# Plain parts of a graph layer: the difference to the gathered rows as a PSUM product on TensorE instead of a subtraction on VectorE

## The chip, the core and the metric

One core of a Trainium2 chip. The metric is the device time of the whole program in microseconds: 2913.64, the median of three runs (2913.59 to 2916.97). The runs of the kernel before and of the changed kernel are compared on the same chip.

## The reference

One graph layer with 12,500 nodes of 128 features and 412,500 edges sorted by destination, followed by a residual and a layer norm:

```python
theta = x[dst] - x[src]
w = sigmoid(relu(theta @ W1 + b1) @ W2 + b2)
agg = segment_sum(w * theta, dst, n_nodes)
indeg = segment_sum(ones, dst, n_nodes)
x = layernorm(x + agg + indeg * (x @ W4 + b4))
```

For an edge the kernel needs relu(y[dst] + b1 - y[src]) with y = x @ W1, its product with W2, a sigmoid, and the weighted sums by destination.

## The kernel before, in words

**Table.** First the kernel computes a table z in DRAM with a row of 256 numbers a node: y = x @ W1 in the first 128, x in the last 128.

**Parts.** Edges are worked on in parts. Parts 0 to 17 are plain parts of 1024 edges each (`PLAIN` = 18, `early_part`); from part 18 on (`part`) 1532 edges make a part, of which up to 1024 are gathered and the rest are "hot" edges, whose source rows TensorE picks out of tables in SBUF (`tabs`, bf16 terms). For a part GpSimd issues eight gathers (`gather`, L404), one for each of eight tiles of 128 edges, into a buffer `zbuf` (128 x 8 x 256). Addresses for parts 0 to 17 come from `src0` (in the profile `src`), those for later parts from `src_i`. Five such buffers go round; part s + 4 is gathered in part s, when the buffer's old part has been weighed.

**One plain part from 4 on.** `spread_y` (L889): TensorE multiplies a one-hot matrix of the destinations (`oh`, or buffers `of` and `wxh` used for it) with the block's y rows (`y_of`), four products of 128x128 for each half of the part, into a PSUM bank (`y` or `pz`; three banks go round). `logits` (L944): VectorE takes PSUM minus gathered rows, half by half, into `zbuf` (L961), then max with 0 times W2 over the whole part, with W2 from the PSUM bank `fix` (L969), then the sum over features (L975). ScalarE makes the one-hots of the destinations within the block's window (`one_hot_w`, L935 and L937), the gate (L988) and the weighted rows `wx` (L999); TensorE adds them up (`add_up`, L1171) for the part before.

**Parts 0 to 3** gather x itself and get their differences by products with -W1 in PSUM; their max and sum (L953, L954) read PSUM, with W2 from SBUF.

**What else lies in parts 4 to 17.** `table_terms` (L1096) builds the hot tables in parts 4 to 9, in turns of ScalarE and TensorE: ScalarE rounds rows to bf16 (L1100), TensorE puts the rows into a bank (L1105, f32, identity), subtracts the rounded ones (L1106) and later the second term (L1111), and ScalarE copies what is left (L1109). There are two banks a turn, `px` and `pd`. The placement of set 0 (`place`), VectorE work in some hundred steps, sorts the edges of parts 18 and on; its steps fill VectorE's time between the plain parts, and all that are left are issued at the start of part 14, ahead of its logits. Its last steps are L693 to L709 (VectorE and ScalarE), the transposes L716 on TensorE and the copy L720 on ScalarE, which writes `src_i`. The first gather of part 18 is issued in part 14.

**Order.** TensorE, VectorE and ScalarE run their instructions in the order of the code (`manual_schedule` with `IN_ORDER`). In plain part s, after the logits of s, comes `spread_y(s + 1)`, then `add_up(s - 1)`, hot products, the gate and weights of s, placement steps, the one-hots for the next pair of parts (L867, L868), and the table terms.

Of the kernel before, what the change touches and what calls it, by code (L numbers as in the profile page):

```python
# [9 lines left out]
F32 = mybir.dt.float32  # L10
# [10 lines left out]
P = 128  # L21
D = 128
K = 8
J = K // 2
# [19 lines left out]
PLAIN = FIRST + MORE  # L44
# [40 lines left out]
def gnn_resnorm(  # L85
# [37 lines left out]
    nc = tc.nc  # L123
# [4 lines left out]
    NF = PLAIN + (E - E1) // CE  # L128
    TAIL = E - E1 - (NF - PLAIN) * CE
    NK = NS // SUB  # L130
    JT = -(-TAIL // (2 * P))
# [14 lines left out]
    const = ctx.enter_context(tc.tile_pool(name="const", bufs=1))  # L146
# [105 lines left out]
    ident = wni[:, 1, :]  # L252
# [6 lines left out]
    b4_r, w2_r = rows["b4_r"], rows["w2_r"]  # L259
# [7 lines left out]

    ident_b = const.tile([P, P], BF16, name="ident_b")
    nident_b = const.tile([P, P], BF16, name="nident_b")
    iota_row = const.tile([P, P], F32, name="iota_row")  # L270
    nc.gpsimd.iota(iota_row, pattern=[[1, P]], base=0, channel_multiplier=0,
                   allow_small_or_imprecise_dtypes=True)
# [16 lines left out]
    for i, t in enumerate(terms):  # L289
        at = slice(i * HALF // 2, i * HALF // 2 + 1)  # L290
# [10 lines left out]
    w2_b = fix[:, WB:WB + D]  # L301
# [22 lines left out]
    def constants():  # L324

        nc.vector.tensor_copy(ident_b, ident)
        nc.vector.tensor_scalar_mul(nident_b, ident, -1.0)
        nc.vector.tensor_scalar_mul(wneg, wts[:, 0, :], -1.0)
        nc.scalar.activation(fix[:, :WB], iota_row[:, :WB], AF.Copy)

        nc.scalar.activation(w2_b, w2_r, AF.Copy)
        for k in range(HR.bit_length() - 1):
            nc.vector.memset(steps_c[:, k:k + 1], ((2 << k) - 1) << FIELD)
        half = const.tile([P, 1], F32, name="half")
        nc.vector.tensor_scalar(half, iota_p, float(HALF), -float(HALF), op0=OP.is_ge, op1=OP.mult)
        nc.vector.tensor_add(half, half, iota_p)
        nc.vector.tensor_scalar(mine, half, float(SW), None, op0=OP.is_lt)
        nc.vector.tensor_scalar(away, half, float(SW), -2.0, op0=OP.is_gt, op1=OP.mult)
        nc.vector.tensor_mul(half, half, mine)
        nc.vector.tensor_sub(away, away, half)  # L340
        nc.vector.tensor_scalar_mul(less, mine, -1.0)

        nodes = const.tile([P, HT], F32, name="nodes")
        node_c = const.tile([P, 1], F32, name="node_c")
        nc.vector.tensor_scalar(node_c, iota_p, float(HT), None, op0=OP.mult)
        nc.vector.tensor_scalar(nodes, iota_row[:, :HT], node_c, None, op0=OP.add)

        most = const.tile([P, 1], F32, name="most")
        nc.vector.memset(most, float(SW + HKL))
        apart = const.tile([P, PM], F32, name="apart")  # L350
        nc.vector.tensor_scalar(apart, iota_row[:, :PM], float(HOT), None, op0=OP.mult)
        return nodes, (apart, most)
# [18 lines left out]
    def pairs(s):  # L371
        return J if s < NF else JT
# [16 lines left out]
    def rows_of(s):  # L389

        if s < NH:
            t = zbuf[s // 2].rearrange("p k d -> p (k d)")[:, (s % 2) * BE:(s % 2 + 1) * BE]
            return t.rearrange("p (k d) -> p k d", d=D)
        return zbuf[(s - NH + NX) % NZ]
# [331 lines left out]
    with tc.manual_schedule(engines={SP}), tc.tile_pool(name="work", bufs=2) as wp, tc.tile_pool(  # L726
        name="ps_y", bufs=2, space=bass.MemoryType.PSUM
    ) as ps_y, tc.tile_pool(
        name="ps_l", bufs=1, space=bass.MemoryType.PSUM
# [15 lines left out]
        def y_tile():  # L745

            turn_y[0] += 1
            if turn_y[0] % 3 == 0:
                return pz.rearrange("p (g d) -> p g d", d=D)
            return ps_y.tile([P, G, D], F32, name="y")  # L750
# [131 lines left out]
        def y_of(s):  # L882

            b, h = divmod(s, SUB)
            if s >= PLAIN:
                return blocks[b]["y2b" if h else "y2"]
            return blocks[b]["y2"][h * HALF:(h + 1) * HALF, :]

        def spread_y(s):  # L889

            d = parts[s]
            d["y"] = []
            for k0 in range(0, K if s < PLAIN else J, J):
                if s < NH:
                    spread_x(s, k0, copy_x(turn_x(s, k0)))
                    continue
                y = y_tile() if s < PLAIN - 1 else ps_y.tile([P, G, D], F32, name="y")
                d["y"].append(y)
                for j in range(J if s < PLAIN else pairs(s)):
                    nc.tensor.matmul(y[:, j, :], d["oh"][:, (k0 + j) * P:(k0 + j + 1) * P],  # L900
                                     y_of(s), start=True, stop=True)

        def turn_x(s, k0):

            px = turning().rearrange("p (k e) -> p k e", e=P)
            for j in range(J):
                nc.tensor.transpose(px[:, j, :], rows_of(s)[:, k0 + j, :], ident)
            return px

        def copy_x(px):  # L910

            xT = next_xT()
            nc.scalar.activation(xT, px, AF.Copy)
            return xT

        def spread_x(s, k0, xT):

            d = parts[s]
            y = y_tile()
            d["y"].append(y)  # L920
            for j in range(J):
                nc.tensor.matmul(y[:, j, :], d["oh"][:, (k0 + j) * P:(k0 + j + 1) * P],
                                 y_of(s), start=True, stop=False)
                nc.tensor.matmul(y[:, j, :], xT[:, j, :], wneg, start=False, stop=True)

        def one_hot_w(s):

            (_, rel, _), i = set_of(s)
            n = pairs(s)
            parts[s]["ow"] = []  # L930
            for k0 in range(0, K if s < PLAIN else J, J):
                ow = wp.tile([P, J, WB], F32, name="ow", bufs=4)
                if NH <= s < PLAIN:
                    for k in range(J):
                        nc.scalar.activation(ow[:, k, :], iota_row[:, :WB], AF.Abs, scale=-1.0,  # L935
                                             bias=rel[:, k0 + k, i:i + 1])
                    nc.scalar.activation(ow, ow, AF.Relu, scale=-1.0, bias=1.0)  # L937
                else:
                    nc.vector.tensor_tensor(
                        ow[:, :n], iota_f.to_broadcast([P, n, WB]),  # L940
                        rel[:, k0:k0 + n, i:i + 1].to_broadcast([P, n, WB]), op=OP.is_equal)
                parts[s]["ow"].append(ow)

        def logits(s):  # L944

            zs = rows_of(s)
            lg = parts[s]["lg"] = wp.tile([P, K, 1], F32, name="lg")
            y = parts[s]["y"]
            if s < NH:
                one_hot_w(s)  # L950
                for i, h in enumerate(y):
                    w2 = w2_r.rearrange("p (o d) -> p o d", o=1).to_broadcast([P, J, D])
                    nc.vector.scalar_tensor_tensor(h, h, 0.0, w2, op0=OP.max, op1=OP.mult)  # L953
                    nc.vector.tensor_reduce(lg[:, i * J:(i + 1) * J, 0], h, AX.X, OP.add)  # L954
                return
            h = zs[:, :, :D]
            n = pairs(s)
            half = h.rearrange("p (i k) d -> p i k d", i=2)[:, :, :n, :]
            if s < PLAIN:
                for i in range(2):  # L960
                    nc.vector.tensor_sub(half[:, i], y[i], half[:, i])  # L961
            else:
                yy = y[0][:, :n, :].rearrange("p (o k) d -> p o k d", o=1)
                nc.vector.tensor_sub(half, yy.to_broadcast([P, 2, n, D]), half)  # L964
            w2 = w2_b.rearrange("p (o d) -> p o d", o=1)
            n = K if s < NF else JT
            tiles = [slice(i, i + n) for i in range(0, K, J if n < K else K)]
            for at in tiles:
                nc.vector.scalar_tensor_tensor(  # L969
                    h[:, at, :], h[:, at, :], 0.0, w2.to_broadcast([P, n, D]),  # L970
                    op0=OP.max, op1=OP.mult)
            if s % SUB == 0:
                one_hot_w(s)
            for at in tiles:
                nc.vector.tensor_reduce(lg[:, at, 0], h[:, at, :], AX.X, OP.add)  # L975
            if s % SUB:
                one_hot_w(s)
# [482 lines left out]
        groups, firsts, i = [], {}, 0  # L1460
# [26 lines left out]
        with after(done[9]):  # L1487
            for b in range(NY):
                window(b)
            plain_one_hots(0)  # L1490
            spread_y(0)
# [9 lines left out]
        def spread_ahead(s):  # L1501

            if s + 2 < NS:
                spread_y(s + 2)
                if PLAIN + AHEAD <= s + 3 < NS:
                    gather(s + 3)
# [265 lines left out]
```

## Time and profile before

| | us |
|---|---|
| median of the runs | 2913.64 |
| the profiled execution | 2916.98 |
| its span, first to last instruction | 2915.2 |
| PE busy (TensorE products) | 2539.6, 87% |
| DVE busy (VectorE) | 2409.2, 83% |
| ACT busy (ScalarE) | 2167.7, 74% |
| POOL busy (GpSimd, the gathers) | 2134.1, 73% |
| stretch from 142 to 299 us (parts 4 to 17): PE, DVE, ACT, POOL busy | 115.1, 132.2, 133.1, 92.6 of 157 |
| mean granted clock of PE in that stretch | 0.84 |

A row of a timeline gives the start and the duration in us, the engine, the line, the operation, out<-in, the shape, the count, and in brackets the idle time before it with the engine and line that ended it. A row of a group gives, behind the count, busy us and the mean in ns, then idle time and its releasers. In the view of waits the figures are the total, the times, and the longest. PE stands for products, PEld for weight loads; one f32 product appears as two instructions. In a table by windows each engine has its busy time with the count of instructions in brackets; the granted clock of PE, the share of the DMA engines and GB/s stand at the end.

### The profile page before, as it was taken

Reading aid. Unit: us, or ns where it says so; the run is one execution under the profiler, and the core shown is the slowest. Engines: PE = TensorE matmul, PEld = TensorE weight load, DVE = VectorE, ACT = ScalarE, POOL = GpSimd, SP = SyncE. Lnnn points to the kernel's source line nnn. Section 1 sums busy time; section 2 is a strip of 40 time slices with the busy share of each in tenths; the row PEclk is TensorE's granted clock in tenths of the full one; section 3 lists DMA queues with packets and bytes.
Section 4 is the critical chain, followed back from the end, with each engine's and each line's share of the span. In section 5 each row is a group of like instructions: output and inputs, shape, how many; then the busy total and the mean of one; then the engine's idle time right before and its main releaser. Section 6 shows DMA issues by size and latency. Waiting matters only on the chain.

```text
span 2915.2 us, 59242 instructions
## 1 busy us (share of the span) xinstructions
PE 2539.6 (87%) x18606; PEld 2005.0 (69%) x18606; DVE 2409.2 (83%) x4413; ACT 2167.7 (74%) x6556; POOL 2134.1 (73%) x2213
## 2 busy tenths in 40 slices
PE   6867899999988999888888889888988899888996
PEld 6646677777776777676766667666776777666775
DVE  7888699998967999988558989988567999888664
ACT  6489877777877778677777767776776877677776
POOL 4556777777777777777777777777777777777774
PEclk8787999999999999999999999999999999999998
DMA  8544555455554555455554555555554555545542
GB/s 276 164 140 130 146 140 137 139 142 140 140 150 133 141 143 140 136 143 136 141 153 132 140 136 143 138 136 140 137 141 134 138 137 143 139 135 142 140 137 76
DMA packets 239330, 413.59 MB, mean 142 GB/s; under 512 B 63423, under 2 KB 147226, under 8 KB 237470
## 3 DMA queue, kind: packets, MB, share of 16 engines
q0 software_dynamic: 105280, 286.93, 35.4%
q1 hardware_dynamic: 131756, 116.40, 15.0%
q10 hardware_dynamic: 1970, 6.40, 0.6%
q8 instruction: 148, 2.42, 0.3%
q14 instruction: 176, 1.44, 0.2%
HBM read 388.57 MB, written 20.94 MB: 140 GB/s over the span
## 4 chain that ended last, share of the span: by engine, by line
PE 39%; ACT 22%; DVE 20%; DMA 10%; issue 8%; POOL 1%; DVEq 0%; ACTq 0%; SPq 0%; POOLq 0%
PE pa L1171 13%; DMA zbuf<-z,src_i 9%; DVE zbuf L964 6%; PE y L900 5%; PE pd L1068 5%; ACT wx L1006 4%; PE px L1132 4%; ACT wxh L1144 3%; PE pz L1118 3%; PE pz L1119 3%; PE pz L1135 3%; ACT oh L879 2%; ACT oh L880 2%; ACT xT L1082 2%; DVE ed L593 1%
## 5 line engine op out<-in xcount | busy, mean ns | idle before, releaser
L404 POOL DMA_INDIRECT zbuf<-z,src_i x2060 | 1991.3, 967 | 634.1 <-issue 247.1
L1006 ACT ACTIVATE wx<-zbuf,wx 128x128 f32<-128x128 f32 x2060 | 630.3, 388 | 0.0
L1171 PE MATMUL pa<-wx,ow 128*104 128x260 f32 (+1 forms) x2284 | 622.5, 390 | 0.0
L900 PEld LDWEIGHTS y<-y,oh 128*128 128x128 f32 (+1 forms) x2156 | 277.7, 198 | 403.1 <-DVE zbuf L964 357.5
L1068 PEld LDWEIGHTS <-tabs 128*128 128x128 bf16 x6360 | 448.9, 100 | 121.8 <-issue 5.9
L1068 PE MATMUL pd<-of,tabs 128*128 128x128 bf16 (+3 forms) x6360 | 530.7, 222 | 0.0
L1124 ACT ACTIVATE hr<-pz 128x512 f32<-128x512 f32 x258 | 152.9, 593 | 495.1 <-PE pz L1119 494.8
L900 PE MATMUL y<-y,oh 128*128 128x128 f32 (+1 forms) x2156 | 314.3, 291 | 214.1 <-DVE zbuf L964 205.3
L964 DVE TENSOR_TENSOR zbuf<-y,zbuf 128x1024 f32<-128x1024 f32 x258 | 314.9, 1220 | 166.2 <-DMA zbuf<-z,src_i 164.6
L1171 PEld LDWEIGHTS pa<-wx,ow 128*104 128x104 f32 x2284 | 338.2, 177 | 40.8
L975 DVE TENSOR_REDUCE lg<-zbuf 128x8 f32<-128x1024 f32 x273 | 329.8, 1208 | 14.1 <-ACT oh L879 0.5
L969 DVE SCALAR_TENSOR_TENSOR zbuf<-zbuf,fix 128x1024 f32<-128x1024 f32 x273 | 331.5, 1215 | 9.3
L1171 PE MATMUL pa<-wxh,owh 128*104 128x130 f32 x2064 | 326.9, 295 | 0.0
L1144 ACT ACTIVATE wxh<-pz,wxh 128x128 f32<-128x128 f32 x1032 | 294.4, 368 | 40.4 <-PE pz L1135 34.4
L1118 PE MATMUL pz<-xT,wni 128*128 128x512 f32 x516 | 279.4, 623 | 3.8 <-ACT wxh L1144 3.8
L1171 PEld LDWEIGHTS pa<-wxh,owh 128*104 128x104 f32 x2064 | 272.1, 185 | 0.0
L1132 PEld LDWEIGHTS px<-w_c,hr 128*128 128x128 f32 x2064 | 264.1, 200 | 9.9 <-ACT hr L1124 9.9
L1132 PE MATMUL px<-w_c,hr 128*128 128x1 f32 x2064 | 263.5, 249 | 7.1 <-ACT hr L1124 7.1
L1119 PE MATMUL pz<-oh,y 128*128 128x512 f32 x516 | 265.4, 596 | 1.0 <-ACT oh L880 1.0
L879 ACT ACTIVATE oh<-to_all,away,mine 128x512 f32<-128x512 bf16 (+1 forms) x257 | 213.6, 831 | 3.1 <-DMA to_all<-off_d 3.1
L1119 PEld LDWEIGHTS pz<-oh,y 128*128 128x128 f32 x516 | 98.6, 191 | 125.5 <-issue 123.7
L1135 PE MATMUL pz<-wni,xT 128*128 128x128 f32 x1032 | 176.0, 297 | 0.0
(308 smaller groups left out, 3675.9 us busy)
## 6 DMA issues: line engine op xcount, KB each, us to landing
to_all<-off_d SPq DMA_DIRECT2D x258, 128.0 KB
zbuf<-z,src_i POOLq DMA_INDIRECT x2060
hot_src<-hot_s SPq DMA_DIRECT2D x228, 128.0 KB
y<-z SPq DMA_DIRECT2D x270, 28.0 KB
xw<-in_x_dram SPq DMA_DIRECT2D x138, 52.0 KB
out_dram<-o SPq DMA_DIRECT2D x138, 52.0 KB
wx<-in_x_dram ACTq DMA_DIRECT2D x12, 512.0 KB
z<-zbuf SPq DMA_DIRECT2D x6, 1024.0 KB
```

Of the source, the lines that this page charges most:

```text
L404: ins = nc.gpsimd.indirect_dma_start(out=rows_of(s)[:, k, :], out_offset=None, in_=z if s >= NH else x, in_offset=IndirectOffsetOnAxis(ap= ...
L900: nc.tensor.matmul(y[:, j, :], d["oh"][:, (k0 + j) * P:(k0 + j + 1) * P], y_of(s), start=True, stop=True)
L964: nc.vector.tensor_sub(half, yy.to_broadcast([P, 2, n, D]), half)
L969: nc.vector.scalar_tensor_tensor(h[:, at, :], h[:, at, :], 0.0, w2.to_broadcast([P, n, D]), op0=OP.max, op1=OP.mult)
L975: nc.vector.tensor_reduce(lg[:, at, 0], h[:, at, :], AX.X, OP.add)
L1006: weighed[0] = nc.scalar.activation(wx[:, k, :D], rows_of(s)[:, k, D:], AF.Copy, scale=wx[:, k, D:D + 1])
L1068: steps_of.append(lambda q=q, i=i, t=t, j=j: nc.tensor.matmul(to[:, q], tabs[:, g, i, q, t, :], of[:, t, q], start=j == 0, stop=j == HT * ...
L1118: nc.tensor.matmul(pz, wneg, xT, start=True, stop=False)
L1119: nc.tensor.matmul(pz, y_of(t), blocks[t // SUB]["oh"][:, BP:], start=False, stop=True)
L1132: nc.tensor.matmul(lgh()[:, t % SUB, q:q + 1], hr[:, at], w2_c, start=True, stop=True)
L1144: nc.scalar.activation(wx[:, q, :D], pz[:, q * P:(q + 1) * P], AF.Copy, scale=wx[:, q, D:D + 1])
L1171: return [lambda i=i, one=one, w=w: nc.tensor.matmul(to if len(w.shape) == 3 else to[:, 0, :], one, w, start=first and i == 0, stop=last a ...
```

## The change

In plain parts 4 to 17 each PSUM bank first gets minus the gathered y rows of that half, by one f32 product of 128x512 with minus the identity (`nident`, a new constant, made once in the opening). The four products with the one-hots then add to it. VectorE's two differences go; max and W2 are taken straight from PSUM, half by half, with W2 from SBUF, and written to `zbuf`. The sum over features stays as it is, as do the parts from 18 on.

```diff
+    nident = const.tile([P, P], F32, name="nident")
...
+        nc.vector.tensor_scalar_mul(nident, ident, -1.0)
...
-                for j in range(J if s < PLAIN else pairs(s)):
+                n = J if s < PLAIN else pairs(s)
+                if s < PLAIN:
+                    nc.tensor.matmul(y, nident, rows_of(s)[:, k0:k0 + J, :D], start=True, stop=False)
+                for j in range(n):
                     nc.tensor.matmul(y[:, j, :], d["oh"][:, (k0 + j) * P:(k0 + j + 1) * P],
-                                     y_of(s), start=True, stop=True)
+                                     y_of(s), start=s >= PLAIN, stop=s >= PLAIN or j == n - 1)
...
-            if s < PLAIN:
-                for i in range(2):
-                    nc.vector.tensor_sub(half[:, i], y[i], half[:, i])
-            else:
+            if s >= PLAIN:
                 yy = y[0][:, :n, :].rearrange("p (o k) d -> p o k d", o=1)
                 nc.vector.tensor_sub(half, yy.to_broadcast([P, 2, n, D]), half)
-            w2 = w2_b.rearrange("p (o d) -> p o d", o=1)
-            n = K if s < NF else JT
+            w2 = (w2_r if s < PLAIN else w2_b).rearrange("p (o d) -> p o d", o=1)
+            n = J if s < PLAIN else K if s < NF else JT
             tiles = [slice(i, i + n) for i in range(0, K, J if n < K else K)]
-            for at in tiles:
+            for i, at in enumerate(tiles):
                 nc.vector.scalar_tensor_tensor(
-                    h[:, at, :], h[:, at, :], 0.0, w2.to_broadcast([P, n, D]),
+                    h[:, at, :], y[i] if s < PLAIN else h[:, at, :], 0.0, w2.to_broadcast([P, n, D]),
                     op0=OP.max, op1=OP.mult)
             if s % SUB == 0:
                 one_hot_w(s)
-            for at in tiles:
+            for at in [slice(0, K)] if s < PLAIN else tiles:
                 nc.vector.tensor_reduce(lg[:, at, 0], h[:, at, :], AX.X, OP.add)
```

The lines of the changed kernel stand up to five further on (L903 is the new product, L905 the products of L900, L971 the maximum of L969).

VectorE in part 4, before: behind a placement step (L596) come the two differences, the maximum over the whole part and the sum.

```order
L596 MATCH_REPLACE ew<-ed,ew 128x767
L961 TENSOR_TENSOR zbuf_177<-y,zbuf_177 128x4x128
L961 TENSOR_TENSOR zbuf_177<-pz,zbuf_177 128x4x128
L969 SCALAR_TENSOR_TENSOR zbuf_177<-zbuf_177,fix 128x8x128
L975 TENSOR_REDUCE lg<-zbuf_177 128x8
L1265 TENSOR_TENSOR xw<-xw,a 104x128
```

The same place now:

```order
L598 MATCH_REPLACE ew<-ed,ew 128x767
L971 SCALAR_TENSOR_TENSOR zbuf_178<-y,w_r 128x4x128
L971 SCALAR_TENSOR_TENSOR zbuf_178<-pz,w_r 128x4x128
L977 TENSOR_REDUCE lg<-zbuf_178 128x8
L1267 TENSOR_TENSOR xw<-xw,a 104x128
```

Two of four instructions a part are of half the width now, and one is gone; the steps around them stand as they did.

TensorE between the table terms of part 6 and those of part 7, before: the products of part 8, the sums of part 6, then the rows of the next turn.

```order
L1111 MATMUL pd<-tabs,nident_b 128x512
L900 MATMUL y<-y_146,oh 128x128 x8
L1183 LDWEIGHTS third
L1183 MATMUL pa<-b_t,third 104x128
L1184 MATMUL pa<-wts,xuT 104x128
L822 MATMUL pa<-wni,xw 128x104
L1171 MATMUL pa<-wx_78,ow 104x130 x8
L1105 MATMUL px<-xT,wni 128x512
L1106 LDWEIGHTS nident_b
L1106 MATMUL px<-tabs,nident_b 128x512
```

Now a wide product stands ahead of each four, and the sums and the turn stand behind both:

```order
L1113 MATMUL pd<-tabs,nident_b 128x512
L903 MATMUL y<-zbuf_177,nident 128x512
L905 MATMUL y<-y_147,oh 128x128 x4
L903 MATMUL y<-zbuf_177,nident 128x512
L905 MATMUL y<-y_147,oh 128x128 x4
L1185 LDWEIGHTS third
L1185 MATMUL pa<-b_t,third 104x128
L1186 MATMUL pa<-wts,xuT 104x128
L824 MATMUL pa<-wni,xw 128x104
L1173 MATMUL pa<-wx_78,ow 104x130 x8
L1107 MATMUL px<-xT,wni 128x512
L1108 LDWEIGHTS nident_b
```

The two new products read `zbuf`, the gathered rows, so that TensorE's queue from here on stands behind the gathers of the next part. ScalarE, GpSimd and SyncE issue the same instructions in the same order as before.

## The prediction

> **What bounds the kernel now.** I read the profile's page first, for the engine that never rests, then the waits of that engine, then its first instruction of the long train of gathers and back from there.
>
> ```profile
> span 2915.2 us, 59242 instructions
> L404 POOL DMA_INDIRECT zbuf<-z,src_i x2060 | 1991.3, 967 | 634.1 <-issue 247.1
> ```
>
> By its busy share POOL (73%) looks like an engine with room. Its longest group of waits between 269.3 and 2888 us (total, times, longest) says otherwise:
>
> ```profile
> POOL zbuf L404 <- issue: 247.1, 811, 0.3
> ```
>
> No wait is longer than 0.3 us, and the other releasers named have the same 0.3, so this is the step from one gather to the next and not a wait. Two rows of POOL's timeline give the ends of the train:
>
> ```profile
> 269.35 0.94 POOL L404 DMA_INDIRECT zbuf<-z,src_i  x1 [6.80 <-ACT src_i L720]
> ...
> 2886.93 0.95 POOL L404 DMA_INDIRECT zbuf<-z,src_i  x1 [0.30 <-issue]
> ```
>
> 2887.88 - 269.35 = 2618.5 us for 2060 gathers, 1.271 us each, without a pause; 27 us of tail follow. The change touches nothing in this train. **So the question is one number: by how much does the 269.35 move**, the moment at which ACT L720 has written src_i, the addresses for part 18 and on. POOL had waited 6.8 us for it; its last plain gather ended at 262.55, so an earlier src_i starts the train earlier one for one up to that.
>
> src_i is the end of the placement: DVE steps (sorting the edges), spread between the plain parts and finished ahead of part 14's logits. DVE, ACT and PE hand work to each other in this stretch, so I look for who came last at each meeting.
>
> **The change part by part: DVE.** A plain part before, in DVE's timeline:
>
> ```profile
> 142.93 0.68 DVE L961 TENSOR_TENSOR zbuf<-y,zbuf 128x512 f32<-128x512 f32 x1
> 143.52 0.68 DVE L961 TENSOR_TENSOR zbuf<-pz,zbuf 128x512 f32<-128x512 f32 x1
> 144.24 1.22 DVE L969 SCALAR_TENSOR_TENSOR zbuf<-zbuf,fix 128x1024 f32<-128x1024 f32 x1
> 145.56 1.22 DVE L975 TENSOR_REDUCE lg<-zbuf 128x8 f32<-128x1024 f32 x1
> ```
>
> and the group nearest to the new form (product in PSUM, weights in SBUF, 512 wide, in parts 0 to 3; shortest, median, longest in ns):
>
> ```profile
> L953 DVE SCALAR_TENSOR_TENSOR y<-y,w_r x5: 687/690/700, 92.8 to 133.6; 128x512 f32<-128x512 f32 x5
> ```
>
> Before: 145.56 - 142.93 = 2.63 us from the difference to the sum. After: two weighted maxima, 0.59 apart as the two differences are, and 0.69 to the sum: 1.28, with the gap of some 0.03 between dependent steps 1.31. That is 1.32 us a part, 18.5 us over 14 parts. Only parts where DVE comes last pay out. ACT's waits for logits show where, as a group and in ACT's timeline:
>
> ```profile
> ACT wx L988 <- DVE lg L975: 7.7, 3, 5.7
> ```
>
> ```profile
> 146.82 0.31 ACT L988 ACTIVATE wx<-lg,b_c 128x8 f32<-128x8 f32 x1 [5.65 <-DVE lg L975]
> ...
> 250.51 0.31 ACT L988 ACTIVATE wx<-lg,b_c 128x8 f32<-128x8 f32 x1 [1.83 <-DVE lg L975]
> ```
>
> Three waits, two of them large. At part 4 ACT waited 5.65, so the whole of that part's saving comes through: **-1.3 us**. From there to 250 us ACT runs on; its other waits are for PE.
>
> The second difference freed its tile 1.28 us after part start, the second maximum does so 1.28 us after; PE gets its banks back as before. The one new operation in the opening (minus the identity, 128x128, once) is a quarter as wide as L953's: 0 to 0.69 us. I take 0, since DVE's placement steps and part 3's logits, which wait for PE's products, lie between it and part 4.
>
> **PE.** It gains 28 products of 128x512 f32. The same shape with the identity as weights stands at L1105, two instructions each:
>
> ```profile
> L1105 PE MATMUL px<-xT,wni x16: 592/592/1057, 149.7 to 224.5; 128*128 128x512 f32 x16
> ```
>
> 1.02 us a product at full clock (153.04 below), 1.9 at half: 2.05 to 3.8 us a part, 29 us or more in all. They now wait for the gathered rows, and what is queued behind them on PE (the sums of the part before, the table terms) waits too. The rows are there. The last gather of part 15 and, in PE's timeline, that part's first product before
>
> ```profile
> 241.62 0.94 POOL L404 DMA_INDIRECT zbuf<-z,src  x1 [0.30 <-issue]
> ```
>
> ```profile
> 269.02 1.16 PE L900 MATMUL pz<-y,oh 64*128 64x128 f32 x8
> ```
>
> stand 27 us apart, and among the waits of L961 in parts 4 to 17 only PE is named, no gather. I cost the new wait at nothing; without that cover each us of late rows would hold up PE's whole queue.
>
> Where does PE's time lie? In parts 4 to 9 ACT and PE build the table terms in turns, and wait for each other:
>
> ```profile
> PE px L1106 <- ACT tabs L1100: 22.3, 7, 4.7
> ...
> ACT tabs L1109 <- PE pd L1106: 8.3, 8, 1.5
> ```
>
> A short and a long turn, first in PE's and then in ACT's timeline:
>
> ```profile
> 152.82 0.38 PE L1106 MATMUL px<-tabs,nident_b 128*128 128x512 bf16 x1 [1.93 <-ACT tabs L1100]
> 153.04 1.02 PE L1105 MATMUL pd<-xT,wni 128*128 128x512 f32 x2
> ...
> 177.91 0.59 PE L1106 MATMUL px<-tabs,nident_b 128*128 128x512 bf16 x1 [4.68 <-ACT tabs L1100]
> 178.29 1.91 PE L1105 MATMUL pd<-xT,wni 128*128 128x512 f32 x2
> ```
>
> ```profile
> 154.31 0.60 ACT L1109 ACTIVATE tabs<-pd 128x512 bf16<-128x512 f32 x1 [0.48 <-PE pd L1106]
> ...
> 180.66 0.60 ACT L1109 ACTIVATE tabs<-pd 128x512 bf16<-128x512 f32 x1 [1.54 <-PE pd L1106]
> ```
>
> The products of the next part come right ahead of these waits, so 2.05 us of the new work goes into 22.3 us of idle time. More than that: after a short wait (1.93) the next product took 1.02 and ACT waited 0.48; after a long one (4.68) it took 1.91 and ACT waited 1.54. The granted clock (seventh figure, PEclk; second is PE's busy time) shows why:
>
> ```profile
> 173.94:177.35 3.41, 0.00 (x0) 0.00 (x0) 3.24 (x6) 3.38 (x6) 2.58 (x3) 1.00 0.35 97
> 177.35:180.76 3.41, 2.85 (x5) 1.06 (x5) 0.54 (x2) 1.20 (x3) 2.50 (x4) 0.50 0.32 95
> 235.38:238.79 3.41, 1.87 (x16) 1.86 (x16) 3.34 (x5) 3.35 (x10) 2.80 (x3) 1.00 0.47 75
> 238.79:242.20 3.41, 3.41 (x18) 3.25 (x17) 3.27 (x7) 3.31 (x12) 2.50 (x4) 0.50 1.00 239
> ```
>
> A stretch of 3.41 us with PE idle is followed by one at half clock. The eight waits of ACT total 8.3 us; at 0.48 each they would be 3.8, so 4.5 us are on offer. With 2.05 us of products inside, even the longest idle time, 4.68, shrinks to 2.6, and hardly any stretch of 3.41 is still empty. But a stretch that was busy for 1.87 us was followed by half clock as well (last two rows), so I count three fifths: **-2.7 us**. [...]
>
> At the first turn (152.82) PE has only 1.93 to spare, 0.6 once ACT comes 1.3 earlier. Part 5's second product waits for part 4's first maximum and costs 1.02 to 1.9, so +0.4 to +1.3, or nothing if the clock stays up and the sums behind it run faster: 0 to 1.3, I take **+0.4**.
>
> **The last stretch, 224 to 269 us.** DVE runs without a pause there, so the logits of part 12 come 2 x 1.32 = 2.6 us earlier against ACT, and the placement's last DVE step 3 x 1.32 = 4.0 (parts 11 to 13). ACT's wait of 1.83 at 250.51 goes, then the 0.31 at 266.37: at best -2.1. PE is what could come late (PE's timeline, then ACT's):
>
> ```profile
> 257.18 2.08 PE L900 MATMUL y<-y,oh 64*128 64x128 f32 x8 [3.22 <-ACT oh L868]
> 259.73 2.04 PE L900 MATMUL y<-y,oh 64*128 64x128 f32 x8 [0.47 <-DVE zbuf L961]
> ...
> 267.91 0.75 PE L716 MATMUL px<-wni,es 128*128 128x128 f32 x4 [0.25 <-ACT es L709]
> ```
>
> ```profile
> 266.37 0.54 ACT L697 ACTIVATE eq<-ed,col 128x256 bf16<-128x256 int32 x1 [0.31 <-DVE ed L693]
> ```
>
> From 257.18 to the transposes of src_i at 267.91 PE pauses for 0.47 and 0.25 only, at half clock. Part 14's first new product fits into the 3.22 us wait. The second costs 1.9 at half clock: 1.9 - 0.47 - 0.25 = +1.2 at the transposes. At full clock it costs 1.02 and everything behind it runs twice as fast, so PE drops out and -2.1 stands. Between -2.1 and +1.2 I take **-1.3**: the first product now fills part of the idle stretch ahead of 257.18, so I go by the rows at full clock, less 0.8, most of one product, which part 12 puts ahead of table products that ACT has to copy before 250.51.
>
> Sum: -1.3 - 2.7 + 0.4 - 1.3 = **-4.9 us**. The profiled execution took 2916.98 (its span of 2915.2 and 1.8 around it), 3.3 above the median of the runs, 2913.64; the shift holds for both: 2912.1 for that execution, **2908.7** on the median.
>
> **Rivals.** A, every turn at full clock: -1.3 - 4.5 - 2.1 = -7.9, 2905.7. For it: no idle time of 3.41 us is left. Against: the stretch with 1.87 us busy. B, the clock falls as before: -1.3 + 1.3 + 1.2 = +1.2 at worst, -1.3 + 0.4 = -0.9 if the last stretch gives and takes nothing; the middle is +0.1, 2913.8. For it: a product in a half-clock stretch only lengthens PE's queue. Against: the empty stretch ahead of 177.35, which the products fill. C, slower: **PE comes last in the table turns**, if a product that reads rows with gaps between them is dear. The dearest row per column is
>
> ```profile
> L1171 PE MATMUL pa<-wx,ow 128*104 128x130 f32 x208 | 31.6, 315 | 0.0
> ```
>
> 2 x 315 ns for 130 columns, by which 512 columns are 2.5 us. Twelve such products in parts 4 to 9 are 29.8 us against 22.3 of waits: +7.5, and 2.5 - 0.7 = +1.8 at the transposes, less 1.3: +8, 2921.6. It decides from 22.3 / 12 = 1.86 us a product on. Against it: the same shape at L1105. D, the change does nothing on the path (another engine ends each meeting at the old time): 2913.6; against it the 5.65 us wait.
>
> **How the numbers follow.** Forecast (between -3 and -7) 0.52, A 0.20, B 0.18, C 0.06, D 0.04. 0.2% is 5.8 us, about what a measurement of this kernel can tell from no change. Faster by more: all of A and two fifths of the forecast, 0.41; slower by more, 0.05; within, 0.54. The range reaches from A, less 1 us for the spread of the runs (2913.59 to 2916.97), to B's upper end (2914.8) and 1 more: 2904.7 to 2915.8. C is left out.
>
> **What would show it.** The train still without a wait over 0.3 us, and its first gather near 264: right about the bound. Part 4's sum near 144.2 and its gate right behind: DVE's term. New products near 1.02 us, ACT's eight waits for the second bank near 5.6 instead of 8.3, fewer half-clock stretches between 160 and 225 us: the clock's term. The transposes of src_i waiting for ACT and not for PE: the last term. Wrong if POOL waits for a buffer inside the train, if PE waits for gathers, or if the train's step of 1.271 us changes.

## The result, and the profile after

| | before | after |
|---|---|---|
| median of 12 runs, us | 2913.93 (2909.87 to 2918.29) | 2906.75 (2899.23 to 2913.62) |
| ratio, 95% interval | | 0.9978 (0.9969 to 0.9986) |
| the profiled execution, us | 2916.98 | 2911.26 |
| first gather of part 18, us | 269.35 | 263.13 |

The change makes the kernel 0.22% faster, 4 to 9 us. First the bound: the train of gathers in POOL's timeline after, and POOL's longest waits between its first and last gather.

```profile
263.13 0.95 POOL L406 DMA_INDIRECT zbuf<-z,src_i  x1 [6.30 <-ACT src_i L722]
...
2882.36 0.95 POOL L406 DMA_INDIRECT zbuf<-z,src_i  x1 [0.31 <-issue]
```

```profile
POOL zbuf L406 <- issue: 248.0, 814, 0.3
```

No wait is longer than 0.3 us here either, the step is 2620.2 / 2060 = 1.272 us, and the train starts 6.22 us earlier. So the question is where ScalarE's way to `src_i` became shorter. I cut that way at four points of ScalarE's timeline that both kernels have: the gate of part 3, the gate of part 4, the first copy from the second bank of the last table turn, and the train's first gather. Before (rows that the prediction doesn't show), then after:

```profile
135.04 0.31 ACT L988 ACTIVATE xT<-lg,b_c 128x8 f32<-128x8 f32 x1 [0.53 <-DVE lg L954]
226.98 0.60 ACT L1109 ACTIVATE tabs<-pd 128x512 bf16<-128x512 f32 x1 [0.48 <-PE pd L1106]
```

```profile
136.42 0.31 ACT L990 ACTIVATE xT<-lg,b_c 128x8 f32<-128x8 f32 x1 [1.04 <-DVE lg L959]
146.94 0.31 ACT L990 ACTIVATE wx<-lg,b_c 128x8 f32<-128x8 f32 x1 [3.01 <-DVE lg L977]
221.24 0.60 ACT L1111 ACTIVATE tabs<-pd 128x512 bf16<-128x512 f32 x1 [0.48 <-PE pd L1108]
262.48 0.66 ACT L722 ACTIVATE src_i<-px 128x256 int32<-128x256 f32 x2 [3.00 <-PE px L718]
```

| stretch, us | before | after | difference |
|---|---|---|---|
| part 3's gate to part 4's gate | 11.78 | 10.52 | -1.26 |
| to the last turn's copy | 80.16 | 74.30 | -5.86 |
| to the train | 42.37 | 41.89 | -0.48 |
| part 3's gate to the train | 134.31 | 126.71 | -7.60 |

Part 3's gate itself came 1.38 later in the profile after. The opening scatters: over the ten profiles in the table of the experiments it lies between 133.1 and 136.9, whatever the kernel. The sums from part 3's gate on do not have this scatter, and I use them from here.

**Part 4.** VectorE's timeline after:

```profile
144.31 0.68 DVE L971 SCALAR_TENSOR_TENSOR zbuf<-y,w_r 128x512 f32<-128x512 f32 x1
144.91 0.68 DVE L971 SCALAR_TENSOR_TENSOR zbuf<-pz,w_r 128x512 f32<-128x512 f32 x1
145.69 1.22 DVE L977 TENSOR_REDUCE lg<-zbuf 128x8 f32<-128x1024 f32 x1
```

From the start to the sum it takes 1.38 us instead of 2.63, and ScalarE's gate stands right behind it (146.94). Three instructions stand where four stood: the two of half width now take the maximum, and the one of full width is gone.

**The table turns.** The waits between 142 and 292 us after (total, times, longest):

```profile
PE px L1108 <- ACT tabs L1102: 13.4, 8, 2.7
...
ACT tabs L1111 <- PE pd L1108: 3.8, 8, 0.5
...
ACT tabs L1111 <- PE px L1108: 3.7, 8, 0.5
```

TensorE's own wait ahead of the turns fell from 22.3 to 13.4, its longest from 4.7 to 2.7, and ScalarE's eight waits for the second bank from 8.3 to 3.8: 0.48 each, in every turn. The clock shows why. In a table by stretches of 3.41 us (second figure PE's busy time, seventh PEclk), two of the emptiest stretches of the turns and what followed:

```profile
175.02:178.43 3.41, 1.67 (x5) 0.67 (x5) 0.00 (x0) 2.47 (x5) 2.51 (x3) 1.00 0.34 96
178.43:181.84 3.41, 3.27 (x13) 1.56 (x12) 2.56 (x10) 3.38 (x15) 2.37 (x3) 1.00 0.84 250
198.91:202.32 3.41, 1.67 (x5) 0.67 (x5) 3.31 (x8) 2.47 (x4) 2.50 (x4) 1.00 0.32 89
202.32:205.74 3.42, 2.48 (x7) 1.00 (x7) 3.18 (x13) 2.72 (x5) 2.35 (x3) 1.00 0.86 262
```

Before, the emptiest had 0.00 to 0.33 (160.28, 173.94, 187.59 and 201.24) and were followed by half clock; now they hold 1.6 to 1.7 us of products and full clock follows. From 131 to 250 us no stretch at half clock is left.

**The last stretch.** TensorE's timeline after, from part 14's first new product to the transposes of `src_i`, and the clock there:

```profile
246.53 1.10 PE L903 MATMUL y<-zbuf,nident 128*128 128x512 f32 x2
249.24 1.31 PE L905 MATMUL y<-y,oh 64*128 64x128 f32 x8 [1.61 <-ACT oh L870]
251.89 2.04 PE L903 MATMUL y<-zbuf,nident 128*128 128x512 f32 x2 [1.35 <-issue]
253.87 2.07 PE L905 MATMUL y<-y,oh 64*128 64x128 f32 x8
...
261.71 0.72 PE L718 MATMUL px<-wni,es 128*128 128x128 f32 x4
```

```profile
246.70:250.11 3.41, 1.80 (x9) 0.97 (x9) 3.24 (x7) 3.38 (x8) 2.50 (x4) 1.00 0.34 100
250.11:253.52 3.41, 2.06 (x5) 0.64 (x3) 3.31 (x8) 3.31 (x13) 2.50 (x4) 0.50 0.39 108
```

Here the clock fell, behind a stretch with 1.80 us of products. The second new product stands behind a pause that ends with VectorE's maximum from bank `y` (251.12 and 0.68 us long) and takes 2.04, the first 1.10; the clock stays at half up to 260.4, and ScalarE waits 3.00 for the transposes where it waited 0.84 before, 2.16 more. Its waits for the logits of part 12 (1.83) and for the placement (0.31) are gone, and so is one of 0.38 for the hot products, so most of these 2.52 us was given back.

### The profile page after: what moved, and what is told of

Its sections match the earlier page's. It is cut to its first block, busy times and chain, and to the rows that moved or that the text cites. A ratio compares the mean times of both kernels' runs of the same rounds, so it can differ in the third digit from the quotient of the medians.

```text
span 2909.5 us, 59390 instructions
## 1 busy us (share of the span) xinstructions
PE 2548.4 (88%) x18662; PEld 1999.4 (69%) x18662; DVE 2392.5 (82%) x4400; ACT 2169.9 (75%) x6556; POOL 2137.2 (73%) x2213
## 4 chain that ended last, share of the span: by engine, by line
PE 37%; ACT 21%; DVE 19%; DMA 10%; issue 7%; POOL 1%; DVEq 0%; SPq 0%; ACTq 0%; POOLq 0%
PE pa L1173 13%; DMA zbuf<-z,src_i 9%; DVE zbuf L966 6%; PE y L905 6%; PE pd L1070 5%; ACT wx L1008 4%; PE px L1134 4%; ACT wxh L1146 3%; PE pz L1120 3%; PE pz L1121 3%; PE pz L1137 3%; ACT oh L881 2%; ACT xT L1084 1%; ACT oh L882 1%; DVE ed L595 1%
## 5 line engine op out<-in xcount | busy, mean ns | idle before, releaser
L1173 PE MATMUL pa<-wx,ow 128*104 128x260 f32 (+1 forms) x2284 | 611.6, 385 | 0.0
L905 PEld LDWEIGHTS y<-y,oh 128*128 128x128 f32 (+1 forms) x2156 | 275.6, 196 | 409.2 <-DVE zbuf L966 365.8
L905 PE MATMUL y<-y,oh 128*128 128x128 f32 (+1 forms) x2156 | 314.8, 291 | 211.4 <-DVE zbuf L966 207.7
L1173 PEld LDWEIGHTS pa<-wx,ow 128*104 128x104 f32 x2284 | 331.6, 173 | 40.4
L971 DVE SCALAR_TENSOR_TENSOR zbuf<-zbuf,fix 128x1024 f32<-128x1024 f32 x259 | 314.4, 1214 | 8.9
```

Source lines behind the costliest of these rows:

```text
L971: nc.vector.scalar_tensor_tensor(h[:, at, :], y[i] if s < PLAIN else h[:, at, :], 0.0, w2.to_broadcast([P, n, D]), op0=OP.max, op1=OP.mult)
L1173: return [lambda i=i, one=one, w=w: nc.tensor.matmul(to if len(w.shape) == 3 else to[:, 0, :], one, w, start=first and i == 0, stop=last a ...
```

## Experiments

The numbers in us. Differences in time are medians against the kernel before in the same comparison; the interval in brackets is that of the ratio times 2914. The last column is the sum that the table above gives -7.60 for.

| kernel | part 3 to 4 | to last turn | to train | part 3 to train, less 134.31 | time, less before |
|---|---|---|---|---|---|
| before | 11.78 | 80.16 | 42.37 | 0 | 0 |
| the change | 10.52 | 74.30 | 41.89 | -7.60 | -7.2 (-9.0 to -4.1) |
| the change again | 10.52 | 74.47 | 41.96 | -7.36 | -4.4 (-8.2 to -2.6) |
| products only | 11.78 | 77.18 | 44.87 | -0.48 | +0.5 (-2.9 to +2.0) |
| VectorE only | 10.53 | 78.74 | 41.65 | -3.39 | -2.4 (-5.2 to 0) |
| parts 4 to 10 | 10.52 | 74.40 | 42.83 | -6.56 | -6.4 (-10.2 to -3.8) |
| parts 11 to 17 | 11.78 | 79.02 | 41.14 | -2.37 | -0.5 (-3.5 to +2.3) |
| warm part 14 | 10.53 | 74.31 | 39.70 | -9.77 | -6.7 (-11.1 to -4.7) |
| warm part 14 again | 10.53 | 74.27 | 39.65 | -9.86 | -8.4 (-14.3 to -6.4) |
| late addresses | 10.53 | 74.29 | 50.70 | +1.21 | +4.5 (+1.5 to +7.6) |

The path lies within the interval of the time in every row but the last, where it misses by 0.3. The intervals are 5 to 8 us wide, so this is a coarse agreement. Each row's path is that of one profile, and that has a scatter too: parts 11 to 17 has the table turns of before, and they took 1.14 us less there than before (79.02 and 80.16). ScalarE's long waits for the second bank stand in other turns there: 0.48 in the fifth turn instead of 1.47, 1.54 in the seventh instead of 0.84.

The change again was expected to have 126 to 127.5 us from part 3's gate to the train, and a time 5 to 9 us below before. The path came at 126.95; the time, 4.4 below, missed.

**The first four runs: a chip on which they tell nothing.** Products alone, VectorE alone, parts 4 to 10 and parts 11 to 17 were first tried there (their edits stand below).

> The kernel before, with the 28 f32 products of 128x512 added on TensorE (two a part, into the bank ahead of the one-hot products, which then overwrite them) and VectorE's differences kept. Theory K (the gain is mostly the clock: the products fill TensorE's idle time ahead of the table turns): ScalarE's eight waits for the second bank fall from 8.3 us to near 4, the stretch from part 4's gate to the last copy of a table turn falls from 80.2 us to 74 to 76, part 4's logits take 2.63 us as before, and the last stretch is 0 to 1.5 us longer than before's 42.4, since TensorE is late there and VectorE gives nothing; the train starts some 4 to 5 us earlier than 269.35, and the time is 4 to 5 us below that of before. Theory V (the gain is VectorE's 18.5 us): no gain, or up to 2 us slower, and the eight waits stay near 8.

> The changed kernel without the 28 products: VectorE takes the maximum straight from the bank, so the subtraction of the gathered rows in parts 4 to 17 is left out of what is computed; TensorE has the work of before. Theory K: the table turns stay as before (eight waits near 8.3 us, 79 to 81 us from part 4's gate to the last turn's copy); part 4 gives 1.3 us and the last stretch up to 2.1 us, since TensorE has no more to do than before: train 3 to 3.5 us earlier, time 2 to 4 us below that of before and above that of the change. Theory V: 6 us or more below before, like the change or better.

> The change in parts 4 to 10 alone, whose products stand ahead of the table turns; parts 11 to 17 in the form of before. Theory K: part 4's 1.3 us and the table turns' 5 to 6 us are there (eight waits below 4.5 us, some 74 to 75 us); the last stretch is that of before, 42 to 43 us: train 6 to 7 us earlier, the time that of the change within 1.5 us. Theory V: half of the gain, about 3 us.

> The change in parts 11 to 17 alone. Theory K: parts 4 to 10 and the table turns as before; only the last stretch can move, and there TensorE comes late at half clock, as in the changed kernel, so 0 to 1.5 us: train near 268 to 269.5, time within 2 us of before. Theory V: half of the gain, about 3 us.

On that chip the kernel before took 4149.08 (4083.6 to 4208.35), and the ratios were 1.0056 (1.0005 to 1.0107), 0.9986 (0.9951 to 1.0021), 0.9960 (0.9911 to 1.0009) and 0.9990 (0.9948 to 1.0033). Between 1000 and 2000 us TensorE's waits in the first of them read:

```profile
PE pd L1072 <- issue: 134.3, 134, 2.6
PE pa L1175 <- issue: 66.6, 78, 2.5
```

An engine that waits for "issue" waits for nothing that the profile shows; such waits of up to 2.6 us stand in the midst of a row of products of one kind, and in the same stretch the train waited 333.2 us for ScalarE's L1010, 112 times and for up to 14.8. The train is not the bound on this chip, so none of the four expectations was tested. What the waits for "issue" come from is not shown. The four kernels were run again on other chips, where before took 2914.

**Products only** (the kernel before, with the 28 products added and overwritten):

```diff
+                if s < PLAIN:
+                    nc.tensor.matmul(y, nident, rows_of(s)[:, k0:k0 + J, :D], start=True, stop=True)
                 for j in range(J if s < PLAIN else pairs(s)):
```

> [...] Theory K (clock): eight waits for the second bank near 4 us instead of 8.3, from part 4's gate to the last copy of a table turn 74 to 76 us instead of 80.2, last stretch 0 to 1.5 us longer than 42.4; train 4 to 5 us earlier than 269.35, time 4 to 5 us below before. Theory V (VectorE's 18.5 us): time that of before or up to 2 us more, table turns 79 to 81 us.

Measured: ratio 0.9998 (0.9990 to 1.0007), no gain, as theory V had it, though the turns did get 2.98 us shorter, which V had not. Theory K fell: it had 4 to 6 us in the turns, and at most 1.5 more in the last stretch. ScalarE's waits for VectorE and its wait for the transposes:

```profile
144.89 0.31 ACT L992 ACTIVATE wx<-lg,b_c 128x8 f32<-128x8 f32 x1 [4.51 <-DVE lg L979]
169.99 0.31 ACT L992 ACTIVATE wx<-lg,b_c 128x8 f32<-128x8 f32 x1 [1.50 <-DVE lg L979]
246.38 0.31 ACT L992 ACTIVATE wx<-lg,b_c 128x8 f32<-128x8 f32 x1 [2.96 <-DVE lg L979]
...
266.29 0.66 ACT L722 ACTIVATE src_i<-px 128x256 int32<-128x256 f32 x2 [2.56 <-PE px L718]
```

The turns are shorter, VectorE's logits are not, so they come last: at part 6 by 1.50 (before 0.23), at part 12 by 2.96 (before 1.83). Behind the first of these one turn still starts at half clock:

```profile
172.16:175.58 3.42, 0.20 (x1) 0.00 (x0) 3.25 (x6) 3.39 (x6) 2.72 (x3) 1.00 0.38 109
175.58:178.99 3.41, 2.77 (x4) 1.06 (x5) 0.40 (x2) 1.20 (x3) 2.50 (x4) 0.50 0.32 90
```

ScalarE's wait for the second bank is 1.54 in that turn and about 0.48 in the others. And at the end TensorE is late at half clock (0.50 from 254.08 to 257.50), with nothing from VectorE against it: +2.5 in the last stretch.

**VectorE only** (the changed kernel without the products; the subtraction of the gathered rows in plain parts 4 to 17 is left out of what is computed):

```diff
-                if s < PLAIN:
-                    nc.tensor.matmul(y, nident, rows_of(s)[:, k0:k0 + J, :D], start=True, stop=False)
...
-                                     y_of(s), start=s >= PLAIN, stop=s >= PLAIN or j == n - 1)
+                                     y_of(s), start=True, stop=True)
```

> VectorE's saving alone once more (no new products; the subtraction of the gathered rows in parts 4 to 17 is left out of what is computed). Theory K: table turns 79 to 81 us, part 4 gives 1.3, the last stretch up to 2.1 since TensorE is not late: train 3 to 3.5 us earlier, time 2 to 4 us below before and above that of the change. Theory V: 6 us or more below before.

Measured: ratio 0.9991 (0.9982 to 1.0000), -2.4 us; theory V fell too. The last stretch gave 0.7 of the 2.1: ScalarE's waits of 1.83 and 0.31 for VectorE are gone, but TensorE ran at half clock behind a stretch with 0.81 us of products, and ScalarE waited 2.01 for its hot products (before 0.38):

```profile
233.50:236.91 3.41, 0.81 (x7) 0.81 (x8) 3.38 (x9) 3.38 (x8) 2.64 (x3) 1.00 0.50 101
236.91:240.33 3.42, 3.42 (x18) 3.19 (x17) 3.25 (x7) 3.33 (x13) 2.67 (x3) 0.50 0.84 163
```

```profile
245.51 0.66 ACT L1082 ACTIVATE xT<-pd 128x448 f32<-128x448 f32 x2 [2.01 <-PE pd L1068]
```

Part 4 gives its 1.25, but the clock still falls behind empty stretches and the turn behind it waits 1.54:

```profile
185.71:189.12 3.41, 0.00 (x0) 0.00 (x0) 3.24 (x12) 3.38 (x10) 2.06 (x2) 1.00 0.52 112
189.12:192.53 3.41, 3.15 (x5) 1.06 (x5) 3.24 (x8) 1.20 (x4) 2.76 (x3) 0.50 0.39 112
```

```profile
192.02 0.60 ACT L1109 ACTIVATE tabs<-pd 128x512 bf16<-128x512 f32 x1 [1.54 <-PE pd L1106]
```

From the two halves came theory J: the products keep the clock in the turns, the shorter logits keep VectorE from coming last behind turns that have become shorter, and only both together give the 5.86. Apart they give 2.98 + 1.42 = 4.40 there, and at the end the products alone cost 2.5. VectorE's 1.42 is hardly more than the 1.14 by which turns that nobody changed differ, so little of it, or none, need be VectorE's.

**Parts 4 to 10, and parts 11 to 17** (`new` takes the place of `s < PLAIN` in all lines of the change; where it is false, VectorE's two differences stay):

```diff
+                new = s <= 10                 # or: 11 <= s < PLAIN
```

> The change in parts 4 to 10 alone. Theory J (both halves of the change are needed together: the products keep the clock, and the shorter logits keep VectorE from coming last behind turns that have become shorter): part 4's term of 1.25 us and all of the turns' 5.9 us are there (74 to 75 us from part 4's gate to the last turn's copy); then VectorE is 2.6 us late at part 12's gate and 3 to 4 at the end of the placement, but TensorE has no new products there, so the train comes 0.5 to 2 us later than with the whole change, counted from part 3's gate (127 to 129 us); time 4.5 to 7 us below before. If the gains simply added up part by part, half: 3 to 4 us.

> The change in parts 11 to 17 alone. Theory J: part 4 and the turns as before (11.8 and 79 to 81 us); the last stretch 41 to 43 us, since ScalarE's waits for logits go and TensorE comes late at half clock in their place: 132.5 to 135 us from part 3's gate to the train, time within 2 us of before. If the gains simply added up part by part: 3 to 4 us below before.

With parts 4 to 10 the turns are at 74.40, all of the gain, and the time is 2907.96, beside 2909.97 for the whole change in the same comparison, which the intervals do not tell apart. Theory J's two lateness terms show in ScalarE's timeline, smaller than expected (2.13 for 2.6, and at the end of the placement 0.48 more), and the transposes are no longer late:

```profile
243.21 0.31 ACT L995 ACTIVATE wx<-lg,b_c 128x8 f32<-128x8 f32 x1 [2.13 <-DVE lg L982]
259.24 0.54 ACT L699 ACTIVATE eq<-ed,col 128x256 bf16<-128x256 int32 x1 [0.48 <-DVE ed L695]
261.55 0.66 ACT L722 ACTIVATE src_i<-px 128x256 int32<-128x256 f32 x2 [0.84 <-PE px L718]
```

Parts 11 to 17 alone: 2913.83 beside 2914.32, nothing that can be told from no change, as J expected; from part 3's gate to the train its profile has 131.94, 0.6 below J's range. Of its 2.37 less than before, 1.14 lie in the turns, which it does not touch, and 1.23 in the last stretch. "Half each" fell. So the seven later parts of the change are worth about 1 us on the path (1.23 alone; 7.60 less 6.56 beside the others) and nothing measurable in time.

**Warm part 14** (the change, and in part 14's first bank more TensorE work that adds nothing; `zero` is a bf16 matrix of zeros):

```diff
+                warm = s == 14 and not k0
+                if warm:
+                    nc.tensor.matmul(y, nident, rows_of(s)[:, k0:k0 + J, :D], start=True, stop=True)
...
+                for j in range(4 if warm else 0):
+                    nc.tensor.matmul(y, zero, tabs[:, 0].rearrange("p i r t d -> p i (r t d)")[:, 0, :P * G],
+                                     start=False, stop=j == 3)
```

> The change, and in part 14's first bank more TensorE work that adds nothing: the product with minus the identity twice (the second overwrites the first), and four bf16 products of 128x512 with a zero matrix behind the one-hot products. Both stand ahead of waits of 1.61 and 1.35 us in the changed kernel, behind which TensorE ran at half clock from 250.1 to 260.4 and ScalarE waited 3.00 us for the transposes of src_i. If that half clock came from those waits, it goes, the transposes start by 260 us, ScalarE's wait falls below 1 us: train 2 to 3 us earlier than in the changed kernel, time 2 to 3 us below it. If it did not, TensorE is later by 0.5 to 1.5 us and so is the train.

> The warm part 14 once more, now beside the change: no half clock between 130 us and the train, ScalarE's wait for the transposes 0.8 us instead of 3.0, from part 3's gate to the train 124 to 125 us; if the train sets the end, the time is 2 to 2.5 us below that of the change. If the time is that of the change within 1 us, something behind the train's start gives the 2 us back.

In both profiles the last stretch is 39.7 us instead of 41.9, and the path from part 3's gate 2.2 to 2.5 us shorter than the change's. (The train's start itself, 259.85 and 259.96, stands 3.3 and 0.3 ahead of the change's 263.13 and 260.26: the opening's scatter.) The second one's clock in the place where it had fallen, and its way to the train:

```profile
245.79:249.20 3.41, 2.66 (x12) 1.35 (x11) 3.24 (x7) 3.38 (x8) 2.50 (x4) 1.00 0.35 100
249.20:252.62 3.42, 2.61 (x12) 1.19 (x13) 3.32 (x8) 3.33 (x12) 2.51 (x4) 1.00 0.38 110
```

```profile
258.53 0.75 PE L720 MATMUL px<-wni,es 128*128 128x128 f32 x4 [1.54 <-ACT es L713]
```

```profile
259.31 0.66 ACT L724 ACTIVATE src_i<-px 128x256 int32<-128x256 f32 x2 [0.84 <-PE px L720]
```

The stretch holds 2.66 us of products instead of 1.80, the clock stays, TensorE waits for ScalarE at the transposes and not the other way round. That the half clock cost some 2.2 us on the path to the train is shown. In time the version was at 2907.29 and 2905.91, the change at 2906.75 and 2909.97; the ratios, 0.9973 (0.9962 to 0.9984) and 0.9965 (0.9951 to 0.9978) against 0.9978 and 0.9982 (0.9972 to 0.9991), overlap. Against the change in the same comparison the second is 4.1 lower, where 2 to 2.5 had been expected. A gain of 2 us over the change is likely, but not shown in time.

**Late addresses** (the change, with 16 copies in place ahead of the transposes):

```diff
         nc.scalar.activation(f, low, AF.Copy)
+        if i == 0:
+            for _ in range(16):
+                nc.scalar.activation(f, f, AF.Copy)
```

> The change with 16 extra ScalarE copies of 128x512 in place, ahead of the transposes of src_i: at 0.61 us each, as the copy ahead of them takes, 9.8 us. If the train of gathers sets the end, its start and the time both come 9.8 us later than with the change (some 2916 to 2917 where before has 2914), and the train keeps its length of 2619 to 2620 us. If something behind it sets the end, the time moves by less than 5 us.

ScalarE's and POOL's timelines:

```profile
258.08 10.55 ACT L714 ACTIVATE es<-es 128x512 f32<-128x512 f32 x16
269.85 0.66 ACT L725 ACTIVATE src_i<-px 128x256 int32<-128x256 f32 x2 [1.22 <-PE px L721]
```

```profile
270.50 0.94 POOL L406 DMA_INDIRECT zbuf<-z,src_i  x1 [15.11 <-ACT src_i L725]
```

The copies took 10.55, and the wait for the late TensorE shrank from 3.00 to 1.22 behind them: 10.55 - 1.78 = 8.8, which is what the sum to the train shows (135.52 - 126.71 = 8.81). The time is 2918.52, 11.8 and 8.6 above the change's two medians. The train sets the end.

## Why the prediction was right, point by point

The forecast was -4.9 (2908.7), measured was -7.2 and, in a second comparison, -4.4; by the path to the train -7.60 and -7.36. The sign, the bound and part 4's term hold; the clock's term was too small, and the last stretch's too large, so that the two errors cancel in part. That the second comparison's -4.4 lies so near to the forecast is chance: on that run's path 7.36 went, not 4.9.

- **The bound.** Right. No wait over 0.3 us in the train, the step 1.272 against 1.271, the late addresses come out at the end.
- **Part 4, -1.3.** Right: 10.52 or 10.53 in all seven profiles with the new form in part 4, 11.78 in all three without.
- **The clock, -2.7, and the first turn, +0.4.** Mechanism right, size wrong: -5.86 (the second profile: -5.69). The step that failed is "But a stretch that was busy for 1.87 us was followed by half clock as well (last two rows), so I count three fifths". Between 150 and 223 us no stretch fell, down to 1.6 us of products, so all of the 4.5 on offer came, as rival A had it. The other 1.2 were not priced: ScalarE's waits for the first bank (4.1 to 3.7) and behind L1111 (0.6 to 0), which had been longer in turns at half clock (up to 0.67 and 0.18 us each, where the turns at full clock had 0.46 and none), and 0.23 at part 6's gate. The +0.4 did not show, as the first turn ran at full clock too: from part 4's gate to the first copy from the second bank it is 7.49 us before and after. (In the second profile the clock fell once, at 141 us, ahead of the first turn, and it is 7.68.) What the prediction did not see is that this term needs VectorE's saving: with the products alone the turns gave half of it, and the whole nothing that can be measured.
- **The new products.** 592 and 622 ns for each of the two instructions in the middle of their groups, as L1105 said; rival C fell. Among their waits no gather is named.

```profile
L903 PE MATMUL pz<-zbuf,nident x18: 592/622/1061, 136.8 to 274.2; 128*128 128x512 f32 x18
```

- **The last stretch, -1.3.** It gave -0.48 and -0.41. Both bounds were at work at once: the -2.1 of VectorE came, and TensorE's lateness at half clock ate it. The step that failed is "so I go by the rows at full clock, less 0.8": the clock fell again behind part 14's first product. Warm part 14 shows what the step would have been worth, -2.7. What the prediction calls "twice as fast" was 1.10 us instead of 2.04 for a wide product and 1.16 instead of 2.07 for the four behind it.
- **The rivals.** A was right about the clock in the turns and wrong for the last stretch. Its sum, -7.9, is nearer to the path's -7.60 than the forecast is, but by luck: it has 4.5 where the turns gave 5.86, and 2.1 where the last stretch gave 0.48. B and D fell with the turns' 74.3.

In these traces stretches of 3.41 us with 0.00 us of products (before at 139.80 and 173.94, VectorE only at 185.71) were followed by half clock. But so were stretches of before that held 0.21 to 0.95 us (160.28, 187.59, 201.24, 218.31), and in part 14 after one with 1.80; in the turns after, those with 1.6 to 1.7 were not. The last section has the counts.

## What to carry to other kernels

When an engine feeds the bound, add up its way to the bound's first instruction, wait by wait, and ask of each wait what else comes last once it is gone: here the two halves of one change gave -0.5 and -3.4 apart and -7.6 together. Work that moved onto a resting TensorE was cheaper than nothing here, where it filled the pause behind which the clock had fallen (the turns became 5.86 us shorter); in part 14, where it left the pause half filled, the second product was paid at half clock (2.04 us instead of 1.10). When a change touches many like places, try it on those ahead of the bound's critical meetings alone: parts 4 to 10 had 6.6 of the 7.6 us.

## What the hardware showed that I had not expected

- **In these profiles no share of busy time alone decided on the clock.** Over nine profiles (those of the table but for late addresses) between 118 and 300 us (398 stretches of 3.41 us at full clock), all 23 with PE busy for a share of at most 0.40 were followed by half clock, of the 76 between 0.40 and 0.66 17 were, and of the 299 above that 4. In the profiles before and after alone it was 7 of 7, 5 of 15, and 1 of 61. The same share goes both ways: behind 1.80 us of 3.41 the changed kernel's clock fell and behind 1.67 it did not, and in the kernel before it fell behind 1.87 (235.38) and 1.52 (252.44) but not behind 1.49 (150.04) and 1.54 (231.96). What decides between 0.4 and 0.66 is open.
- **Three of the four are at one place in the opening, and what follows is shifted.** In the changed kernel's profile a busy stretch was followed by half clock:

```profile
123.82:127.23 3.41, 3.14 (x17) 2.08 (x15) 3.27 (x7) 0.60 (x1) 2.50 (x4) 1.00 0.35 101
127.23:130.64 3.41, 3.41 (x16) 3.38 (x16) 3.27 (x6) 1.66 (x5) 2.80 (x3) 0.50 0.38 112
```

The same place in the kernel before, with the same 3.14 us busy, stayed at full clock (122.74 to 129.56). It happened in three profiles, where the stretch began at 122.9 to 124.3, and in none where it began earlier. In these three, part 3's gate stands at 135.5 to 136.9 us, in the other seven at 133.1 to 135.3. The stretches lie differently against the program in each run (the changed kernel's second profile has one that begins at 120.98), so the same kernel meets the clock differently. How much of the scatter of some 10 us between runs comes from this is not shown.
- **The train's own length scatters.** 2618.0 to 2623.1 us for the same 2060 gathers over ten profiles, without a pause over 0.5 us in any; a difference of 2 us at its start cannot be read from the end of one execution.
